# Quantized experts: two key and value banks in each of eight middle turns, copied by ScalarE, which also scales six tiles of tokens

## The chip, the cores and the metric

The kernel runs on one core of one Trainium2 chip. It is one program with one launch. The metric is device time in microseconds (us) of a whole execution, the median of several runs. A core has five engines that work side by side, each of which takes its own instructions in the order of the program: TensorE (PE in the profile, with its weight loads apart as PEld), VectorE (DVE), ScalarE (ACT), GpSimd (POOL) and SyncE (SP, which here only starts transfers). [...]

## The reference

Two decoder layers, each an attention-like block, a cross attention and a feed-forward block with a layer norm behind each. The change touches the first block of layer 0, a mixture of eight quantized experts plus one shared expert over 2048 tokens of width 256, and the place where some work of layer 1 (its keys and values) is done early.

```python
def activation_quant(x):
    scale = 127.0 / jnp.clip(jnp.max(jnp.abs(x), axis=-1, keepdims=True), 1e-05)
    return jnp.clip(jnp.round(x * scale), -128, 127) / scale
def weight_quant(w):
    scale = 1.0 / jnp.clip(jnp.mean(jnp.abs(w)), 1e-05)
    return jnp.clip(jnp.round(w * scale), -1, 1) / scale
def bitlinear(x, w):
    xn = rmsnorm(x, BIT_EPS)
    return activation_quant(xn) @ weight_quant(w).T
def bit_mlp(x, gate_proj_w, down_proj_w):
    gate, y = jnp.split(bitlinear(x, gate_proj_w), 2, axis=-1)
    return bitlinear(jax.nn.silu(gate) * y, down_proj_w)
# layer 0, first block
shared_out = bit_mlp(x_flat, shared_gate_w, shared_down_w)
...
routed = routed + w_keep[:, None] * bit_mlp(x_flat, expert_gate_w[e], expert_down_w[e])   # e in 0..7, top 2, capacity 320
# layer 1, cross attention, from the context alone
K = (key_value @ W_k); V = (key_value @ W_v)
```

(`activation_quant` and `weight_quant` stand in the reference inside a straight-through form, whose value is the one shown.)

## The kernel before

`stage0` computes the quantized experts. Its order is written out by hand (`manual_schedule`): every engine gets its instructions in the order in which the Python code calls them.

**Tiles and turns.** The stage works on 36 tiles of 128 token rows: 14 tiles of the shared expert, 20 of the routed experts (five for each pair of experts, gathered by an indirect transfer), and 2 more shared ones. The loop at L689 runs turns n = 0 to 37, and in one turn three tiles are in flight. In turn n:

- PE multiplies the tokens of tile n + 2 by the gate and up weights (`gated`, L503, into `ps_g` and `ps_y`, two buffers each), multiplies the hidden rows of tile n - 1 by the down weights (`down`, L557, into the single `ps_o`), and transposes the hidden rows of tile n (`turn`, L546, into `ps_t`, two buffers);
- ACT copies the transposed rows of tile n - 1 out (`turned`, L550, tile `m_hT`), computes silu for tile n + 1 (`silu`, L511, tile `m_sg`), and sums the squares of tile n (`squares`, L520);
- DVE multiplies silu by the other half (`hidden`, L516, tile `m_h`), takes the largest magnitude (L524), two small steps (L529, L530), rounds (`rounded`, L541, tile `m_r`), and writes tile n - 2 out (`done`, L564 or L570; ACT does it at L568 for odd expert tiles);
- the token rows of a new group are transposed by PE (L472) and copied by ACT (L473, tile `xqT`).

**Jobs.** Each turn also has a list of jobs, all of them behind the work above. Expert e is prepared in six of these turns from n = 2 + 3e on (`made_in`): sums of its weights on ACT (L223, L231) and DVE (L225), a small matmul (`total`, L235), scaling on ACT (L244), rounding on DVE (L247, L250). Turns 0 to 3 quantize token tiles 8 to 15, two tiles a turn, by `quantized` (L284 scales and rounds one tile into `m_q`, L285 writes it to `xq` as bf16). Turns 2 to 8 hold the pieces of the routing, a long row of small DVE instructions (L321 to L429).

**Banks of keys and values.** `made_early` (L575) is a generator. Each `next` on it gives PE one PSUM bank of layer 1's keys or values to compute (L2108 for the 16 key banks, L2115 for the 12 value banks, 28 in all), always into the same tile `ps_k`, of which there is one buffer (`bufs=1`). `out_of` (L583) copies the bank into a tile `kv` (L585) and SP sends that to DRAM (L586). In the loop, from turn 4 on, one bank a turn is made just ahead of `gated`, and its copy stands behind `down`: on ACT in turns 4 to 10 and where n % 3 is 1, on DVE in the other turns behind 10. The last bank is made in turn 31. The copy on ACT stands in program order behind `turned`, `silu` and `squares` of its turn.

Of the kernel before, what the change touches and what calls it, by code (L numbers as in the profile page):

```python
# [13 lines left out]
AF = mybir.ActivationFunctionType  # L14
ALU = mybir.AluOpType
# [9 lines left out]
MAGIC = 12582912.0  # L25
# [93 lines left out]
def stage0(K, early, ahead, late, late_dram, context):  # L119
# [6 lines left out]
    tc, nc = K.tc, K.nc  # L126
    x = K.x
    with ExitStack() as ctx:
# [21 lines left out]
        def load_half():  # L150
            what, i = halves[len(w_kv)]
            w_kv.append(K.new(wp, [P, KD, 512], F32, "w_kv", bufs=2))
            wide = K.ins["l1x_W_" + what].rearrange("(k p) n -> p k n", p=P)
            nc.sync.dma_start(w_kv[-1], wide[:, :, 512 * i:512 * i + 512])
# [9 lines left out]
        for g in range(4):  # L164
            t = K.new(wp, [P, KD, 4 * P], F32, "q", bufs=5)
# [9 lines left out]
        magic = K.new(keep, [P, 1], F32, "magic")  # L175
# [34 lines left out]
        def weights(e):  # L210
# [48 lines left out]
        ss, am, rs_bit, rs_gate, a, step, sc = (  # L259
            K.new(keep, [P, NB], F32, t) for t in ("ss", "am", "rs_bit", "rs_gate", "a", "step", "sc")  # L260
        )
# [19 lines left out]

        def quantized(b):
            t = K.new(work, [P, D], F32, "m_q", bufs=3)
            nc.vector.tensor_scalar(t, x[b], sc[:, b:b + 1], MAGIC, ALU.mult, ALU.add)  # L284
            nc.vector.tensor_scalar(xq[:, b, :D // 2].bitcast(BF16), t, MAGIC, None, ALU.subtract)  # L285


# [178 lines left out]
        def tokens(g, t0):  # L466

            m = min(4, g.n - t0)
            pt = K.new(ps, [P, 8, P], BF16, "ps_t")
            for t in range(m):  # L470
                for k in range(KD):
                    nc.tensor.transpose(pt[:, 2 * t + k, :], g.rows[t0 + t][:, k * P:(k + 1) * P], K.identb)  # L472
            return lambda: nc.scalar.copy(g.xqT[:, 2 * t0:2 * (t0 + m), :], pt[:, :2 * m, :])  # L473
# [18 lines left out]
        def scaled(g):  # L492
            nc.vector.tensor_tensor(g.s1, g.factor, g.backs[0], ALU.mult)
# [3 lines left out]
        def gated(n):  # L497
            g, t = tiles[n]
            pg[n], py[n] = (K.new(ps, [P, FF], F32, tag) for tag in ("ps_g", "ps_y"))
            for j, dst in enumerate((pg[n], py[n])):  # L500
                for part, w in g.use[t]:
                    for k in range(KD):
                        nc.tensor.matmul(  # L503
                            dst[part, :], g.xqT[:, 2 * t + k, part], w[0][:, k, FF * j:FF * j + FF],
                            start=(k == 0), stop=(k == KD - 1),
                        )

        def silu(n):
            g, t = tiles[n]
            sg[n] = K.new(work, [P, FF], F32, "m_sg", bufs=3)  # L510
            nc.scalar.activation(sg[n], pg[n], AF.Silu, scale=g.s1[:, t:t + 1])  # L511

        def hidden(n):
            g, t = tiles[n]
            h[n] = K.new(work, [P, FF], F32, "m_h", bufs=2)
            nc.vector.scalar_tensor_tensor(h[n], py[n], g.s1[:, t:t + 1], sg[n], ALU.mult, ALU.mult)  # L516

        def squares(n):
            g, t = tiles[n]
            nc.scalar.activation(sg[n], h[n], AF.Square, accum_out=g.ss[:, t:t + 1])  # L520

        def largest(n):
            g, t = tiles[n]
            nc.vector.tensor_reduce(g.am[:, t:t + 1], h[n], AX.X, ALU.max, apply_absolute_value=True)  # L524

        def step_of(n):
            g, t = tiles[n]
            at = slice(t, t + 1)
            nc.vector.tensor_scalar(g.step[:, at], g.am[:, at], 1e-9, 1.0 / 127.0, ALU.max, ALU.mult)  # L529
            nc.vector.reciprocal(g.s2[:, at], g.step[:, at])  # L530

        def factor(n):
            g, t = tiles[n]
            at = slice(t, t + 1)
            K.rsqrt(small, g.rs[:, at], g.ss[:, at], 1.0 / FF, 1e-8, "m_rt")
            nc.gpsimd.tensor_scalar(g.s3[:, at], g.rs[:, at], g.step[:, at], g.backs[1][:, at], ALU.mult, ALU.mult)

        def rounded(n):
            g, t = tiles[n]
            r[n] = K.new(work, [P, FF], F32, "m_r", bufs=2)  # L540
            nc.vector.tensor_scalar(r[n], h[n], g.s2[:, t:t + 1], MAGIC, ALU.mult, ALU.add)  # L541

        def turn(n):
            pt[n] = K.new(ps, [P, 4, P], F32, "ps_t")
            for k in range(4):
                nc.tensor.transpose(pt[n][:, k, :], r[n][:, k * P:(k + 1) * P], K.ident)  # L546

        def turned(n):
            hT[n] = K.new(work, [P, 4, P], BF16, "m_hT", bufs=3)
            nc.scalar.activation(hT[n], pt[n], AF.Identity, bias=unmagic)  # L550

        def down(n):
            g, t = tiles[n]
            po[n] = K.new(ps, [P, D], F32, "ps_o", bufs=1)
            for part, w in g.use[t]:
                for k in range(4):
                    nc.tensor.matmul(po[n][part, :], hT[n][:, k, part], w[1][:, k, :], start=(k == 0), stop=(k == 3))  # L557

        def done(n):
            g, t = tiles[n]  # L560
            s = g.s3[:, t:t + 1]
            if g.shared:
                b = g.i + t
                nc.vector.scalar_tensor_tensor(x[b], po[n], s, x[b], ALU.mult, ALU.add)  # L564
                return
            y = K.new(work, [P, D], F32, "y", bufs=3)
            if t % 2:
                nc.scalar.mul(y, po[n], s)  # L568
            else:
                nc.vector.tensor_scalar(y, po[n], s, None, ALU.mult)  # L570
            at = PAIR * g.i + P * t
            nc.sync.dma_start(y_dram[at:at + P, :], y)


        def made_early():  # L575
            for i in range(4):
                yield from context.early(
                    *halves[i], w_kv[i], ctxT, lambda: K.new(ps, [P, 512], F32, "ps_k", bufs=1),
                )
                if i < 2:  # L580
                    load_half()

        def out_of(bank, to, on_vector):  # L583
            t = K.new(work, [P, 512], F32, "kv", bufs=3)
            (nc.vector.tensor_copy if on_vector else nc.scalar.copy)(t, bank)  # L585
            nc.sync.dma_start(to, t)  # L586


# [5 lines left out]
        for b in range(4):  # L594
            quantized(b)
# [10 lines left out]
        for b in range(4, 8):  # L606
            quantized(b)
# [54 lines left out]
        for b in range(8, 12):  # L662
            job((b - 8) // 2, quantized, b)
# [21 lines left out]

        turned_tokens, made_banks = None, made_early()
        for n in range(N + 2):  # L689
            old, mid, now = 1 < n, 0 < n <= N, n < N  # L690
            if mid:
                turned(n - 1)
            if turned_tokens is not None:
                turned_tokens()
                turned_tokens = None
            if n in first_jobs:
                first_jobs[n]()
            if now:
                hidden(n)
            if n in then_jobs:  # L700
                then_jobs[n]()
            if n + 1 < N:
                silu(n + 1)
            if now:
                largest(n)
                squares(n)
                step_of(n)
                rounded(n)
            if old:
                done(n - 2)  # L710
            bank = next(made_banks, None) if n >= 4 else None
            if n + 2 < N:
                gated(n + 2)
            if mid:
                down(n - 1)
                factor(n - 1)
            if bank is not None:
                out_of(*bank, n > 10 and n % 3 != 1)
            for f, args in jobs.get(n, ()):
                f(*args)  # L720
            if n + 2 in starts:
                scaled(starts[n + 2])
            if n + 3 in starts:
                prepare(starts[n + 3])
                turned_tokens = tokens(starts[n + 3], 0)
            if n + 2 in starts and starts[n + 2].n > 4:
                turned_tokens = tokens(starts[n + 2], 4)
            if now:
                turn(n)
        assert next(made_banks, None) is None  # L730
# [2055 lines left out]
```

## Time and profile before

| what | value |
| --- | --- |
| median of 3 runs | 1367.72 us (1364.27 to 1368.48) |
| profiled execution, device time | 1373.0 us |
| its span, first to last instruction | 1371.2 us |
| stage of this change in the span | about 0 to 197 us |
| busy in the span | PE 89%, PEld 62%, DVE 60%, ACT 49%, POOL 35% |
| mean granted TensorE clock | 0.961 |
| bank copies (L585) | 14 on ACT, 8.2 us busy, 586 ns each; 14 on DVE, 9.5 us busy, 681 ns each |
| scaling of a token tile (L284) | 16 on DVE, 5.6 us busy, 348 ns each |

The turns can be found by the 36 `m_h` instructions of L516 on DVE: turn 0 begins at 23.81 us, turn 4 at 51.23, turn 9 at 84.02, turn 17 at 120.34, turn 24 at 150.88, turn 32 at 180.46 and turn 35 at 190.27. In a timeline a row gives start, length, engine, line, operation, what is written and read, how many instructions were merged, and in brackets how long the engine was idle before it and what ended that wait. The length of a row is longer than the distance to the next row of the same engine, since instructions are pipelined: for what an engine can do in a time, distances between starts count.

### The profile page before, as it was taken

How to read it: one execution, taken by the hardware profiler on the slowest of the kernel's cores; microseconds unless marked ns; L12 is line 12 of the kernel's file. 1: busy time of each engine (PE TensorE's matmuls, PEld its weight loads, DVE VectorE, ACT ScalarE, POOL GpSimd, SP SyncE). 2: the span in 40 equal slices, each digit the busy share in tenths (PEclk: the TensorE clock that was granted, in tenths of full speed). 3: DMA queues.
4: the chain of work that ended last, by engine and by line, in shares of the span. 5: the costliest groups of instructions: out<-in, count | busy, mean ns of one | idle time of the engine just before them, and what ended most of it. 6: DMA issues, size and time to landing. Idle time of an engine off the chain costs nothing.

```text
span 1371.2 us, 19329 instructions
## 1 busy us (share of the span) xinstructions
PE 1216.6 (89%) x6815; PEld 848.0 (62%) x6815; DVE 823.1 (60%) x1753; ACT 672.6 (49%) x1736; POOL 473.1 (35%) x632
## 2 busy tenths in 40 slices
PE   3678888889978898989798999998989999999994
PEld 1456444666654566766666888877776665666653
DVE  7799977989976898856555566676334111211115
ACT  5779864768965566636225566556431111111110
POOL 3256547658872566530052323323102000000003
PEclk9899988989999999989799999999999999999998
DMA  8458324201100311112000211210023322133002
GB/s 297 157 169 285 137 62 103 28 1 55 47 32 33 100 62 47 47 39 77 0 1 32 75 65 62 79 64 30 1 68 133 107 73 100 43 108 108 10 8 75
DMA packets 63121, 103.55 MB, mean 76 GB/s; under 512 B 11920, under 2 KB 41712, under 8 KB 62768
## 3 DMA queue, kind: packets, MB, share of 16 engines
q1 hardware_dynamic: 60848, 96.76, 20.8%
q0 software_dynamic: 2176, 5.55, 1.9%
q8 instruction: 54, 0.88, 0.3%
q14 instruction: 43, 0.35, 0.1%
HBM read 81.74 MB, written 16.35 MB: 72 GB/s over the span
## 4 chain that ended last, share of the span: by engine, by line
PE 55%; DVE 29%; ACT 7%; issue 4%; POOL 3%; DMA 2%; SPq 0%; DVEq 0%; POOLq 0%; ACTq 0%
PE ps_y L2616 8%; PE ps_m L2605 8%; PE ps_g L2605 7%; PE ps_m L2161 4%; DVE acc L1356 3%; ACT s L2263 2%; PE ps_t L2283 2%; PE ps_m L2292 2%; DVE cT L1365 2%; DVE m L2257 1%; DVE s L2253 1%; DVE s L915 1%; PE ps_t L2272 1%; PE ps_s L2250 1%; DVE m L922 1%
## 5 line engine op out<-in xcount | busy, mean ns | idle before, releaser
L2610 DVE TENSOR_TENSOR h<-h,ps_m 128x512 f32<-128x512 f32 x60 | 41.3, 688 | 228.4 <-PE ps_m L2605 228.4
L82 POOL TENSOR_SCALAR ln_t<-ln_mv 128x1 f32<-128x1 f32 (+2 forms) x76 | 15.0, 197 | 442.3 <-DVE ln_mv L90 296.2
L2263 ACT ACTIVATE s<-s,m 128x128 f32<-128x128 f32 x256 | 99.3, 390 | 69.0 <-DVE m L2257 69.0
L2609 ACT ACTIVATE h<-ps_g 128x512 f32<-128x512 f32 x60 | 35.8, 597 | 171.0 <-PE ps_g L2605 171.0
L2605 PE MATMUL ps_g<-xin,w 128*128 128x512 f32 x224 | 106.3, 592 | 0.0
L2605 PE MATMUL ps_m<-xin,w 128*128 128x512 f32 x224 | 105.3, 592 | 0.0
L2616 PE MATMUL ps_y<-w,h 128*128 128x256 f32 x448 | 97.8, 379 | 0.0
L2616 PEld LDWEIGHTS ps_y<-w,h 128*128 128x128 f32 x448 | 85.1, 190 | 14.6 <-issue 3.3
L2267 POOL TENSOR_TENSOR s<-s,t 128x1024 f32<-128x1024 f32 x32 | 60.7, 1898 | 86.7 <-DVE t L2266 86.7
L927 ACT ACTIVATE s<-s,m 128x128 f32<-128x128 f32 x256 | 83.2, 394 | 12.3 <-DVE m L922 12.3
L2605 PEld LDWEIGHTS ps_m<-xin,w 128*128 128x128 f32 x224 | 42.5, 190 | 51.4 <-issue 50.2
L2605 PEld LDWEIGHTS ps_g<-xin,w 128*128 128x128 f32 x224 | 42.0, 190 | 46.4 <-issue 45.0
L2161 PE MATMUL ps_m<-xT,half 128*128 128x256 f32 x256 | 62.7, 390 | 1.8 <-issue 1.3
L2617 ACT COPY y<-ps_y 128x256 f32<-128x256 f32 x30 | 11.2, 372 | 104.7 <-PE ps_y L2616 73.9
L2253 DVE TENSOR_TENSOR s<-ps_s,hide 128x1024 f32<-128x1024 f32 x32 | 39.1, 1223 | 36.1 <-PE ps_s L2250 36.0
L2292 PE MATMUL ps_m<-half,oT 128*128 128x256 f32 x256 | 59.3, 385 | 0.0
L1356 DVE SCALAR_TENSOR_TENSOR acc<-ps_m,l1a_conv_w,acc 128x508 f32<-128x508 f32 (+2 forms) x72 | 53.2, 739 | 3.0 <-ACT acc L1349 1.3
L2161 PEld LDWEIGHTS ps_m<-xT,half 128*128 128x128 f32 x256 | 47.7, 195 | 8.4 <-issue 2.0
L2292 PEld LDWEIGHTS ps_m<-half,oT 128*128 128x128 f32 x256 | 47.4, 190 | 7.5
L2263 ACT ACTIVATION_READ_ACCUMULATOR s<-s,m 128x1 f32 x256 | 48.1, 188 | 0.0
L83 POOL TENSOR_TENSOR ln_rs<-ln_t,mhalf 128x1 f32<-128x1 f32 (+2 forms) x76 | 45.6, 600 | 6.3
L1347 PE MATMUL ps_m<-xnT,l1a_in_proj 128*128 128x512 f32 x96 | 45.5, 596 | 0.4 <-ACT y L1317 0.4
(543 smaller groups left out, 3063.7 us busy)
## 6 DMA issues: line engine op xcount, KB each, us to landing
w<-in_w_gate_dram SPq DMA_DIRECT2D x9, 1024.0 KB, 7.2
csb<-cs_dram SPq DMA_DIRECT2D x16, 512.0 KB, 3.7
w<-in_l1f_gateT_dram SPq DMA_DIRECT2D x14, 512.0 KB, 4.4
w<-in_l1f_upT_dram SPq DMA_DIRECT2D x14, 512.0 KB, 5.8
w<-in_l1f_downT_dram SPq DMA_DIRECT2D x14, 512.0 KB, 4.7
k<-kv SPq DMA_DIRECT2D x20, 256.0 KB, 2.4
v<-kv SPq DMA_DIRECT2D x20, 256.0 KB, 2.1
ring<-k SPq DMA_DIRECT2D x10, 512.0 KB, 4.2
```

The source lines that it names most:

```text
L83: return self.nc.gpsimd.tensor_tensor(out, t, self.mhalf[: out.shape[0], :n], ALU.pow)
L927: nc.scalar.activation(at, at, AF.Exp, bias=m[h][:, i:i + 1])
L1347: nc.tensor.matmul(pc, w.inp[:, k, at:at + P], xnT[g][:, k, :], start=(k == 0), stop=(k == KD - 1))
L1356: nc.vector.scalar_tensor_tensor(accv[:, :, j:], pcv[:, :, :P - j], w.conv[:, c, TAPS - 1 - j:TAPS - j], accv[:, :, j:], ALU.mult, ALU.add,)
L2161: nc.tensor.matmul(pq[:, j, :], wt[k][:, at], src[:, k, :], start=(k == 0), stop=(k == KD - 1))
L2253: nc.vector.tensor_tensor(half(b, j), pss.rearrange("p r c k -> p (r c) k"), hide.unsqueeze(1).to_broadcast([P, 8, P]), ALU.add,)
L2263: nc.scalar.activation(at, at, AF.Exp, bias=m[j][:, i:i + 1], accum_out=t[j][:, i:i + 1])
L2267: nc.gpsimd.tensor_tensor(half(b, j), half(b, j), t[j].unsqueeze(2).to_broadcast([P, 8, P]), ALU.mult)
L2292: nc.tensor.matmul(py[b], oT[b][:, c, :], w.o[c // 4][:, c % 4, :], start=(c == 0), stop=(c == NC - 1))
L2605: nc.tensor.matmul(ps[:, j, :], m[k][:, c * P:(c + 1) * P], self.r.xin[:, k, e, cols], start=(k == 0), stop=(k == KD - 1),)
L2610: nc.vector.tensor_tensor(h, h, pu, ALU.mult)
L2616: nc.tensor.matmul(pd, rows(c), w.down[c // 4][:, c % 4, :], start=(c == 0), stop=(c == FI // P - 1))
```

## The change

Three things are changed.

1. `quantized` takes its first instruction (scale and round) to ACT for tiles 8, 9, 10, 11, 14 and 15. The second instruction, which reads its result, stays on DVE. Tiles 0 to 7, 12 and 13 are as before.
2. `out_of` always copies on ACT.
3. At the end of each of the turns 9 to 16, ahead of `turn(n)`, a second bank is made. Its copy stands in turn n + 1, on ACT, behind `squares` and `done` and ahead of that turn's first bank. The 28 banks end in turn 23.

```diff
         def quantized(b):
             t = K.new(work, [P, D], F32, "m_q", bufs=3)
-            nc.vector.tensor_scalar(t, x[b], sc[:, b:b + 1], MAGIC, ALU.mult, ALU.add)
+            if b < 8 or b in (12, 13):
+                nc.vector.tensor_scalar(t, x[b], sc[:, b:b + 1], MAGIC, ALU.mult, ALU.add)
+            else:
+                nc.scalar.activation(t, x[b], AF.Identity, scale=sc[:, b:b + 1], bias=magic)
             nc.vector.tensor_scalar(xq[:, b, :D // 2].bitcast(BF16), t, MAGIC, None, ALU.subtract)
-        def out_of(bank, to, on_vector):
+        def out_of(bank, to):
             t = K.new(work, [P, 512], F32, "kv", bufs=3)
-            (nc.vector.tensor_copy if on_vector else nc.scalar.copy)(t, bank)
+            nc.scalar.copy(t, bank)
             nc.sync.dma_start(to, t)
-        turned_tokens, made_banks = None, made_early()
+        turned_tokens, made_banks, more = None, made_early(), None
         for n in range(N + 2):
...
             if old:
                 done(n - 2)
+            if more is not None:
+                out_of(*more)
             bank = next(made_banks, None) if n >= 4 else None
             if n + 2 < N:
                 gated(n + 2)
             if mid:
                 down(n - 1)
                 factor(n - 1)
             if bank is not None:
-                out_of(*bank, n > 10 and n % 3 != 1)
+                out_of(*bank)
             for f, args in jobs.get(n, ()):
                 f(*args)
...
             if n + 2 in starts and starts[n + 2].n > 4:
                 turned_tokens = tokens(starts[n + 2], 4)
+            more = next(made_banks) if 9 <= n < 17 else None
             if now:
                 turn(n)
```

## The prediction

> **What bounds the stage now.** First the busy time of the engines in three stretches: turns 9 to 16, 17 to 23, 24 to 31.
>
> ```profile
> core 0: us, PE busy (x) PEld busy (x) DVE busy (x) ACT busy (x) POOL busy (x), PEclk, DMA share, GB/s
> 84.05:120.27 36.22, 31.63 (x193) 23.15 (x194) 34.29 (x78) 32.21 (x51) 24.59 (x45) 1.00 0.77 249
> 120.27:150.16 29.89, 26.83 (x150) 16.50 (x149) 28.51 (x64) 27.96 (x46) 17.43 (x34) 1.00 0.66 227
> 150.16:180.45 30.29, 28.18 (x143) 14.43 (x141) 28.67 (x63) 23.32 (x43) 15.50 (x35) 1.00 0.32 112
> ```
>
> DVE is 95% busy in each, but nobody has room: in turns 9 to 16 PE has 4.6 us free of 36.2 and ACT 4.0. Only behind 150 us has ACT slack (7.0 us). Next one turn in order of time, turn 15 (its `m_h` is at 111.39), with the row that follows on each engine:
>
> ```profile
> 110.67 1.89 PE L2108 MATMUL ps_k<-ctxT,w_kv 128*128 128x256 f32 x8
> 111.04 0.68 ACT L550 ACTIVATE m_hT<-ps_t,unmagic 128x512 bf16<-128x512 f32 x1
> 111.61 0.69 ACT L511 ACTIVATE m_sg<-ps_g,m_s 128x512 f32<-128x512 f32 x1
> 112.19 0.64 ACT L520 ACTIVATE m_sg<-m_h 128x512 f32<-128x512 f32 x1
> 112.40 0.59 PE L503 MATMUL ps_g<-q,xqT 128*128 128x512 bf16 x2
> 112.80 1.24 ACT L244 ACTIVATE w<-w,magic,w_s 128x1024 f32<-128x1024 f32 x1
> 112.83 0.59 PE L503 MATMUL ps_y<-q,xqT 128*128 128x512 bf16 x2
> 114.07 0.68 DVE L585 COPY kv<-ps_k 128x512 f32<-128x512 f32 x1
> 114.20 0.60 PE L557 MATMUL ps_o<-q_d,m_hT 128*128 128x256 bf16 x4 [0.77 <-DVE x L564]
> 114.63 0.60 PE L546 MATMUL ps_t<-ident,m_r 128*128 128x128 f32 x4
> 115.21 1.97 PE L2108 MATMUL ps_k<-ctxT,w_kv 128*128 128x256 f32 x8
> 115.27 0.69 ACT L550 ACTIVATE m_hT<-ps_t,unmagic 128x512 bf16<-128x512 f32 x1 [1.23 <-PE ps_t L546]
> 117.22 0.59 ACT L585 COPY kv<-ps_k 128x512 f32<-128x512 f32 x1
> ```
>
> The reader is to see that the bank is PE's first work of a turn. It starts 0.58 us behind the transposes of the turn before (114.63, then 115.21) and waits for nobody, because `ps_k` was emptied a whole bank's time earlier, at 114.07. The bank fills PE while ACT does `m_hT`, `m_sg` and the squares. The turn's length of 4.53 us (36.22 over 8) is DVE's.
>
> **Part 1, two banks a turn.** There is one `ps_k`. In the new order PE runs, in a turn: bank, `gated`, `down`, second bank, `turn`. ACT runs `turned`, `silu`, `squares`, copy of the second bank of the turn before, copy of this turn's bank, jobs. So PE's first bank of turn n waits for a copy that stands behind `squares(n)`, which stands behind `turned(n-1)`, which needs the transposes that PE does only behind the second bank. The two engines wait for each other in a ring, and what waits on PE behind that first bank is everything: `gated`, `down`, and so DVE and ACT of the next turn. Once round, in distances between starts from the rows above:
>
> - first bank 1.73 (110.67 to 112.40); `gated` 0.86 (twice 112.40 to 112.83); `down` 0.43 (114.20 to 114.63); second bank 1.73; `turn` until `turned` can start 0.64 (114.63 to 115.27): PE's part, 5.39 us;
> - `turned` 0.57, `silu` 0.58, `squares` with its read 0.61 (111.04, 111.61, 112.19, 112.80); the copy 0.59; release to PE 0.05 (114.15, the end of DVE's L564, to 114.20): ACT's part, 2.40 us, in which PE stands still.
>
> Together 7.79 us a turn. The second bank itself doesn't wait: ACT's copy of the first can start when the bank is 2.01 old (115.21 to 117.22) and ends at 2.60, PE comes to the second at 3.02. ACT's job (at most 2.0 us, L244) lies beside PE's `gated` to `turn`, and DVE (34.3 us for the eight turns) beside all of it; these are covered. Eight rounds, from the bank of turn 9 to that of turn 17, are 62.3 us. To it come pieces that now hide and then lie in the ring: copies of token rows on ACT (L473) in turns 10, 12, 13 and 17, by their distances 0.47, 0.89, 0.25, 0.89; their transposes on PE (L472) 0.22, 0.45, 0.12, 0.44; one `y` (L568) 0.36 in turn 17. Sum 4.1. So 66.4 us instead of 36.2: **+30.2 us**. Bounds: +6.6 if the waits vanished and PE's own 5.35 us a turn set it (2 x 1.73 + 0.86 + 0.43 + 0.44, and 0.15 for token rows; 8 x 5.35 - 36.2), and the +30.2, with some 3 us either way, if the ring holds. I take +30.2, because the program's order leaves no other way round.
>
> The transfers: each copy brings one to SP's queue (2.4 us to landing, 256 KB). A copy needs the `kv` buffer of three copies before, 1.5 turns or 11.7 us earlier. In turn 11 SP issues 14 loads for later stages in a row, which took 9.2 us (97.29 to 106.46 on SP); the second bank of that turn queues behind them, and 9.2 + 2.4 is just under 11.7. I cost it at 0; without that cover it is 1 us, once.
>
> **The clock.** A PE that waits may be slowed:
>
> ```profile
> 52.03 1.01 PE L503 MATMUL ps_y<-q_s,xqT 128*128 128x512 bf16 x2 [2.91 <-DVE m_h L516]
> 76.68 2.92 PE L2108 MATMUL ps_k<-ctxT,w_kv 128*128 128x256 f32 x8
> ```
>
> The first, behind a wait of 2.91 us, took 1.01 instead of 0.59. The second took 2.92 instead of 1.97 and had only waits of 1.68 and 1.76 us in the 5 us before. From 52 to 84 us PE was busy 22.52 of 32 and the granted clock was 0.85; from 84 to 120 it was 1.00. The ring leaves PE still 2.40 of 7.79 us, 31%, as much as the stretch at 0.85. Bounds for eight turns: 0, and 5.39/0.85 - 5.39 = 0.95 a turn, 7.6 us. I take **+4 us**, the middle, as the waits at 52 to 84 were uneven and some longer.
>
> [...]
>
> **Part 2, all copies on ACT.** 14 copies leave DVE, 0.60 each in distances (109.67 to 110.27), 8.4 us; 28 are now on ACT at 0.48 (117.22 to 117.70). Four of the moved ones stood in turns 11 to 16, where the ring decides: 0. Five stood in turns 17 to 23, and there ACT (27.96 of 29.89 busy) takes 5 x 0.48 = 2.4 for the 3.0 that DVE loses: I take 0, bounds -2.4 and +1.9. In turns 24 to 31 no bank is left, and DVE, which ran without a gap, loses five copies, 3.0, and the one wait of 0.41 us that a copy had for its bank (165.51): **-3.4 us**. The last turns have DVE's own row of work (2.36 us from 187.91 to 190.27) as a floor, which isn't reached.
>
> **Part 3, six tiles scaled on ACT.** DVE loses 6 x 0.39 = 2.3 us (26.38 to 26.75, 30.45 to 30.83). But DVE takes its instructions in order too, and the L285 that stays waits for ACT.
>
> ```profile
> 30.24 0.29 DVE L285 TENSOR_SCALAR xq<-m_q 128x256 bf16<-128x256 f32 x1
> 31.04 1.39 DVE L264 TENSOR_REDUCE am<-x 128x1 f32<-128x256 f32 x4
> 31.43 0.20 ACT L520 ACTIVATION_READ_ACCUMULATOR m_sg<-m_h 128x1 f32 x1
> 45.09 0.28 DVE L331 TENSOR_REDUCE best<-pr 128x16 f32<-128x128 f32 x1 [1.13 <-ACT pr L328]
> 48.05 0.19 ACT L520 ACTIVATION_READ_ACCUMULATOR m_sg<-m_h 128x1 f32 x1
> ```
>
> Turn 0: ACT is free at 26.24, both tiles are ready by 27.0, nothing lost. Turn 1: the scaling stands on ACT behind the squares (31.43). With ACT's 0.41 us for such a tile and 0.30 between two (L268 at 23.47), tile 11 is ready at 32.23, DVE's second L285 runs at 32.28 and L264 at 32.49 instead of 31.04: +1.45. DVE runs without a gap from 27.56 to the routing's first step at 36.69, and PE's next transposes wait for that step, so it stays. Turn 3: the scaling stands behind squares at 48.05, moved by the same 1.45 to 49.50; tile 15 is ready at 50.3, DVE goes on at 50.56, where L331 now starts at 45.09. Behind L331 DVE has the routing without a gap until the `m_h` at 51.23, for which PE and ACT wait. So **+5.5 us** in all; bounds -2.3 (ACT never late) and +6.5.
>
> **Sum.** 30.2 + 4.0 - 3.4 + 5.5 = +36.3. The profiled execution took 1373.0 (span 1371.2 and 1.8 around it), so 1409.3 for such a one; the median shown is 5.3 us lower, 1367.7, and the forecast goes by it: **1404 us**. All later stages need the stage's result and move along.
>
> **Rivals.**
> - *The engines' own work sets it, not the ring.* Turns 9 to 16 at PE's 5.35 us: +6.6, with +5.5 and -3.4 makes +8.7, 1376. For it: PE and ACT are nearly full already. Against: it needs ACT's copy ahead of `turned`, and it stands behind.
> - *Relief of DVE decides, and it is faster.* DVE was 95% busy; it loses 8.4 + 2.3 = 10.7 us: 1357. It decides if PE's idle time in turns 9 to 16 takes eight more banks, 8 x 1.73 = 13.8 us. Against: there were 4.6 us.
> - *The clock halves all through the ring.* PE's 5.39 us double: 8 x 5.39 = 43 instead of 4, 1443. For it: the row at 76.68. Against: from 59 to 84, with many waits of 1 to 2 us, only the 3.4 us around that bank were slow.
> - That the banks aren't doubled: the built order shows both, with the wait for ACT on each.
>
> **How the numbers follow.** Forecast 0.82, engines' work 0.08, clock 0.06, relief 0.04. Range: front +3.5 to +6.5, ring +27 to +32, clock 0 to +7.6, turns behind -5.8 to -1.5, together +25 to +45, that is 1392 to 1412; widened by the spread of the runs (1364.3 to 1368.5) and a little of the clock's case, 1390 to 1417. Within 0.3% (4 us), about what a measurement of this kernel can tell from no change, lies a quarter of the relief's case: same 0.01, faster 0.03, slower 0.96.
>
> **What would show it.** The bank of turn 17 some 66 us behind that of turn 9; PE's first bank of a turn with an idle time of 2.4 us ended by ACT `kv`; DVE idle in these turns, about 30 us more; `L331` near 50.5, behind a wait for ACT `m_q`; turns 24 to 31 about 3 us shorter. Wrong would be: no PE wait for `kv`, or a turn near 5.4 us.

## The result, and the profile after

| | before | after |
|---|---|---|
| median of 4 runs, us | 1368.10 (1364.27 to 1368.53) | 1410.80 (1408.22 to 1414.47) |
| ratio, 95% interval | | 1.0321 [1.0291, 1.0350] |
| profiled execution, us | 1373.0, span 1371.2 | 1410.84, span 1408.8 |
| bank of turn 9 starts, us | 84.05 | 89.62 |
| from there to the bank of turn 17 | 36.22 | 76.07 |
| from there to the transposes of turn 23 | 29.45 | 30.50 |
| from there to the transposes of turn 31 | 32.39 | 30.42 |
| from there to stage 1's first matmul | 15.54 | 15.37 |
| stage 1's first matmul starts, us | 197.65 | 241.98 |

The change made the kernel 42.7 us slower; 1404 had been forecast. The stage is 44.33 us longer in the two traces. Where stages 1 to 5 run the same instructions, they still differ from execution to execution: from stage 1's first matmul to the end of the span it is 1173.6 us before and 1166.8 after, and 1164.5 to 1176.4 over all twelve profiles of this study. A change of a few us inside this stage is therefore read at stage 1's first matmul (below: the end of the stage); the runs' times confirm it only when it is larger.

In the code after, a line behind L287 stands 3 lower and one behind the loop of turns' first edit up to 6 lower than before: the bank's copy is L588, `turn` L549, `turned` L553, `silu` L514, `squares` L523, `hidden` L519, a bank L2114 or L2121. The busy time by stretch of the kernel after, with the columns as before, for turns 9 to 16, 17 to 23 and 24 to 31:

```profile
89.62:165.69 76.07, 54.48 (x236) 35.75 (x236) 37.53 (x83) 41.82 (x69) 24.86 (x47) 0.88 0.56 174
165.69:196.62 30.93, 29.42 (x136) 15.34 (x137) 21.83 (x50) 26.69 (x45) 16.39 (x33) 0.91 0.45 151
196.62:225.81 29.19, 18.52 (x118) 10.90 (x116) 25.51 (x58) 22.51 (x41) 13.96 (x35) 0.88 0.17 53
```

DVE, 95% busy before, is busy for 37.53 of 76.07 us in the first stretch, and no engine is full there: PE has 72%, ACT 55%. A stretch in which everybody has time is one in which they wait for each other. PE's clock fell from 1.00 to 0.88 in the same rows. The round of turn 15 in order of time, on PE and ACT (start, length, engine, line; in brackets the idle time before):

```profile
143.20 0.60 PE L549 MATMUL ps_t<-ident,m_r 128*128 128x128 f32 x4
143.84 0.69 ACT L553 ACTIVATE m_hT<-ps_t,unmagic 128x512 bf16<-128x512 f32 x1 [1.45 <-PE ps_t L549]
144.42 0.68 ACT L514 ACTIVATE m_sg<-ps_g,m_s 128x512 f32<-128x512 f32 x1
144.99 0.63 ACT L523 ACTIVATE m_sg<-m_h 128x512 f32<-128x512 f32 x1
...
145.60 0.58 ACT L588 COPY kv<-ps_k 128x512 f32<-128x512 f32 x1
146.24 2.50 PE L2121 MATMUL ps_k<-w_kv,ctxT 128*128 128x512 f32 x4 [2.44 <-ACT kv L588]
148.53 1.06 PE L506 MATMUL ps_g<-q,xqT 128*128 128x512 bf16 x2
...
149.38 1.06 PE L506 MATMUL ps_y<-q,xqT 128*128 128x512 bf16 x2
150.23 0.97 PE L560 MATMUL ps_o<-q_d,m_hT 128*128 128x256 bf16 x4
151.04 1.88 PE L2121 MATMUL ps_k<-w_kv,ctxT 128*128 128x512 f32 x4
152.76 0.60 PE L549 MATMUL ps_t<-ident,m_r 128*128 128x128 f32 x4
```

ACT's wait ends with PE's transposes, and PE's wait ends with ACT's copy: the ring. What ACT does between (143.84 to 146.24) are 2.40 us, in which PE stands still. Soon behind the wait PE works at half speed (the granted clock is 0.50 from 147.57 to 150.98): from 148.53 to 149.38 are 0.85 us for `ps_g`, where the same two matmuls need 0.43 elsewhere, and the bank of 146.24 takes 2.29 us, where the one of 107.99, behind an equal wait but at full clock, took 1.83. That is the second part of the loss.

The waits of the same kernel from 89 to 166 us (waiting engine, line, for whom: total, times, longest); before, PE had no wait for `kv` in these turns:

```profile
PE ps_k L2114 <- ACT kv L588: 11.6, 5, 3.4
PE ps_k L2121 <- ACT kv L588: 8.5, 3, 3.7
```

Part 3 of the change, on ACT and DVE in turns 1 and 3:

```profile
30.20 0.20 ACT L523 ACTIVATION_READ_ACCUMULATOR m_sg<-m_h 128x1 f32 x1
30.29 1.08 ACT L287 ACTIVATE m_q<-x,magic,sc 128x256 f32<-128x256 f32 x2
30.92 0.29 DVE L288 TENSOR_SCALAR xq<-m_q 128x256 bf16<-128x256 f32 x1 [1.51 <-ACT m_q L287]
...
49.16 1.08 ACT L287 ACTIVATE m_q<-x,magic,sc 128x256 f32<-128x256 f32 x2
49.78 0.29 DVE L288 TENSOR_SCALAR xq<-m_q 128x256 bf16<-128x256 f32 x1 [5.99 <-ACT m_q L287]
...
50.51 0.27 DVE L334 TENSOR_REDUCE best<-pr 128x16 f32<-128x128 f32 x1
```

DVE stands before L288 until ACT, whose scaling is queued behind the squares, has delivered. The routing's L334 begins at 50.51; it began at 45.09.

### The profile page after: what moved, and what is told of

The parts are those of the page before. It is cut to its first block, busy times and chain, and to the rows that moved or that the text cites. A ratio compares the mean times of both kernels' runs of the same rounds, so it can differ in the third digit from the quotient of the medians.

```text
span 1408.8 us, 19332 instructions
## 1 busy us (share of the span) xinstructions
PE 1226.5 (87%) x6815; PEld 853.1 (61%) x6815; DVE 813.4 (58%) x1733; ACT 682.7 (48%) x1756; POOL 470.3 (33%) x632
## 4 chain that ended last, share of the span: by engine, by line
PE 51%; DVE 21%; ACT 8%; issue 4%; POOL 3%; DMA 1%; DVEq 0%; POOLq 0%; ACTq 0%
PE ps_y L2622 7%; PE ps_m L2611 7%; PE ps_g L2611 7%; PE ps_m L2167 4%; DVE acc L1362 3%; ACT s L2269 2%; PE ps_t L2289 2%; PE ps_m L2298 2%; DVE cT L1371 2%; DVE m L2263 1%; DVE s L2259 1%; DVE s L921 1%; PE ps_t L2278 1%; PE ps_s L2256 1%; PE ps_g L1986 1%
## 5 line engine op out<-in xcount | busy, mean ns | idle before, releaser
L2114 PE MATMUL ps_k<-ctxT,w_kv 128*128 128x256 f32 x128 | 39.3, 462 | 11.6 <-ACT kv L588 11.6
```

What stands on the lines that cost most here:

```text
L2114: nc.tensor.matmul(bank[:, 2 * P * j:2 * P * (j + 1)], w[:, k, cols], ctxT[:, k, G * g * P:G * (g + 1) * P], start=(k == 0), stop=(k == KD ...
```

## The experiments

Theory: three things cost time. The ring (PE's first bank of a turn behind a copy that stands late in ACT's order), PE's half clock behind the ring's waits, and the scaling that makes DVE wait for ACT. Rivals: too much work for some engine, a clock that has nothing to do with the waits, or transfers.

| kernel | median, us (lowest to highest) | kernel before, same chip | ratio, 95% interval | bank of turn 9 | to bank of turn 17 | clock in that stretch | end of the stage |
|---|---|---|---|---|---|---|---|
| before | | | | 84.05 | 36.22 | 1.00 | 197.65 |
| after | 1410.80 | 1368.10 | 1.0321 [1.0291, 1.0350] | 89.62 | 76.07 | 0.88 | 241.98 |
| e1 | 1377.38 (1370.66 to 1381.91) | 1370.23 | 1.0046 [1.0021, 1.0070] | 91.48 | 36.41 | | 205.42 |
| e2 | 1369.42 (1366.44 to 1373.33) | 1370.23 | 1.0001 [0.9979, 1.0023] | 82.75 | 35.34 | 1.00 | 195.70 |
| e3 | 1410.46 (1402.07 to 1413.21) | 1371.28 | 1.0276 [1.0228, 1.0325] | 84.18 | 77.53 | 0.86 | 238.16 |
| e4 | 1389.24 (1385.44 to 1397.84) | 1370.23 | 1.0158 [1.0116, 1.0200] | 90.65 | 53.41 | 0.97 | 218.91 |
| e5 | 1396.93 (1388.31 to 1398.47) | 1370.23 | 1.0172 [1.0131, 1.0214] | 88.45 | 58.77 | 1.00 | 220.03 |
| e6 | 1411.11 (1407.60 to 1411.92) | 1371.28 | 1.0304 [1.0261, 1.0347] | 89.98 | 74.27 | 1.00 | 237.76 |
| e8 | 1385.92 (1379.50 to 1386.70) | 1371.28 | 1.0108 [1.0070, 1.0145] | 90.08 | 48.96 | 1.00 | 213.86 |
| e9 | 1367.93 (1366.07 to 1370.81) | 1371.28 | 0.9983 [0.9961, 1.0005] | 84.03 | 36.44 | 1.00 | 196.93 |
| e10 | 1402.20 (1400.10 to 1405.20) | 1370.60 | 1.0233 [1.0211, 1.0256] | 90.11 | 67.89 | 1.00 | 230.94 |
| e11 | 1405.92 (1405.07 to 1406.66) | 1370.60 | 1.0256 [1.0239, 1.0273] | 89.71 | 67.89 | 1.00 | 232.71 |

**e1, the scaling alone.** The kernel before, with the first hunk of the diff and nothing else.

> The kernel before with only the scaling of tiles 8 to 11, 14 and 15 on ScalarE; banks and copies as before. Theory (VectorE takes its instructions in order and waits for ScalarE): the m_h of turn 4 comes 5.4 us later than the 51.23 of before, and the whole is 5.5 us slower, 1373.6 against 1368.1. Rival (VectorE is the bound and is relieved of six instructions): 2.3 us faster, 1365.8.

Measured: 0.46% slower, [+0.21, +0.70], that is 2.9 to 9.6 us, and the end of the stage 7.8 us later, 7.4 of them by the bank of turn 9 (5.57 in the kernel after). DVE waits 2.16 us for `m_q` in turn 1 and 5.99 in turn 3. The `m_h` of turn 4 comes at 58.63, 7.40 us later where 5.4 was expected; in the kernel after it is 5.38. One pair of profiles is not good to better than some 3 us here: up to the bank of turn 9 all kernels with the scaling run the same instructions, and so do those without, and that bank comes between 88.45 and 91.48 us in the eight profiles with it and between 82.75 and 84.18 in the four without. The means are 6.3 us apart. So the scaling costs somewhat more than the theory asked, though it takes work from the fullest engine.

**e2, the copies alone.** The kernel before, with all copies on ACT, still one bank a turn.

```diff
-                out_of(*bank, n > 10 and n % 3 != 1)
+                out_of(*bank, False)
```

> The kernel before with all 28 bank copies on ScalarE and still one bank a turn. Theory: no ring can form, since a bank is copied in its own turn and the next one starts a turn later, so VectorE's relief counts where ScalarE has room: 1 to 5 us faster, 1363 to 1367 against 1368.1, most of it behind turn 24. Rival (ScalarE is the bound of the middle turns, and copies there cost as much as they relieve): within 2 us of before, or slower.

Measured: no difference within 0.23%, which is 3.2 us, so a gain of 1 or 2 us is neither shown nor excluded. In its trace the stage ends 2 us earlier, but 1.3 of them are there at the bank of turn 9, ahead of anything that was changed. ACT is 32.00 of 32.00 us busy from 118 to 150: what DVE lost there, ACT became. As a cause of the slowdown the copies are out.

**e4, the second bank's copy at once.** The kernel after, with this copy behind its own bank instead of a turn later.

```diff
-            if more is not None:
-                out_of(*more)
...
-            more = next(made_banks) if 9 <= n < 17 else None
+            if 9 <= n < 17:
+                out_of(*next(made_banks))
```

> The changed kernel with one call moved: the second bank's copy is called right behind its matmuls, so on ScalarE it stands ahead of the next turn's m_hT instead of behind its squares. Same work on every engine. Theory (a ring of waits between TensorE and ScalarE): a turn of 9 to 16 falls from 9.5 us to about 5.7 (5.39 of TensorE and a wait of 0.48), eight turns with the token rows about 47 us instead of 76, the whole 1382 against 1410.8. Rival (two banks a turn are simply too much work for TensorE or ScalarE): no gain, above 1405.

Measured: 21.6 us below the kernel after, with the same work on every engine. So it was not too much work; it was one copy's place in ACT's order. A turn is 5.72 us where nothing else happens (97.59 to 103.31), and PE waits 0.2 to 0.3 us for a copy. But 47 us for the eight turns and 1382 for the whole had been expected, and 53.41 and 1389.24 came. One turn stood out, in the timeline of this kernel:

```profile
112.33 2.83 SPq L75 DMA_DIRECT2D dist_scale<-in_dist_scale_dram  x1
117.49 4.64 SPq L589 DMA_DIRECT2D k<-kv  x4
121.20 0.58 ACT L588 COPY kv<-ps_k 128x512 f32<-128x512 f32 x1 [3.74 <-DMA k<-kv]
121.84 3.60 PE L2113 MATMUL ps_k<-ctxT,w_kv 128*128 128x256 f32 x8 [2.27 <-ACT kv L588]
```

SP issues turn 11's 14 loads one after another (to 117.49, one of them 2.83 us); the copies' transfers queue behind them, and ACT's copy has no free `kv` buffer until one lands. With turns of 7.79 us three copies were 11.7 us, enough; with 5.7 us they are 8.6, and the cover is gone. PE then waits 2.27 us and the bank takes 3.60 us, where the others of these turns take 1.88 to 1.99.

**e8, the same with five buffers.** `bufs=3` in `out_of` becomes `bufs=5`.

> The kernel in which the second bank is copied right behind its own matmuls (1389.24 us), with five buffers instead of three for the copies on their way to memory. Theory (one copy there waited 3.74 us for the transfer of three copies before, held up behind fourteen loads on SyncE's queue, and TensorE then 2.27 us and a bank at half clock): no such wait, no slow bank, bank of turn 9 to bank of turn 17 in 46 to 50 us beside 53.41, the run 1383 to 1387 us. Rival (the wait only moves, or ScalarE's own work is the bound there): 52 us or more, the run at 1388 or above.

Measured: no wait for a transfer, no slow row, 48.96 instead of 53.41 us for the eight turns, and a median 3.3 us lower, all as expected. The times alone would not show it, since the intervals of the two ratios overlap; the traces settle the cause of that one stall.

**e5, the copy one place behind `turned`.** The kernel after, with the copy of the second bank moved ahead of `silu` and `squares`, but still in the next turn.

```diff
             if turned_tokens is not None:
                 turned_tokens()
                 turned_tokens = None
+            if more is not None:
+                out_of(*more)
...
-            if more is not None:
-                out_of(*more)
```

> The changed kernel with the second bank's copy moved only ahead of silu and squares, still behind m_hT and the token rows. Theory: the ring's part on ScalarE falls from 2.40 to about 1.21 us (0.57 + 0.59 + 0.05), 8 x 1.19 = 9.5 us less, and with shorter waits most of the 8.7 us of half clock goes too: 1392 to 1398 against 1410.8. Rival (too much work): no gain, above 1405.

Measured: in the expected range. In rounds without token rows PE waits 1.25 us, 1.15 to 1.19 less than 2.40 to 2.44, which is `silu` and `squares` (0.57 and 0.61); a turn is 6.70 us (125.49 to 132.19). And there is not one slow row in the ring, not even behind the 2.17 us of turn 12:

```profile
110.89 1.99 PE L2114 MATMUL ps_k<-ctxT,w_kv 128*128 128x256 f32 x8 [2.17 <-ACT kv L588]
132.19 1.99 PE L2121 MATMUL ps_k<-w_kv,ctxT 128*128 128x512 f32 x4 [1.25 <-ACT kv L588]
```

**e6, PE kept busy while it waits.** The kernel after, with four f32 matmuls ahead of the first bank in turns 10 to 17. They go into `ps_g`, and `gated` overwrites them.

```diff
             if more is not None:
                 out_of(*more)
+            if more is not None:
+                pg[n + 2] = K.new(ps, [P, FF], F32, "ps_g")
+                for k in range(4):
+                    nc.tensor.matmul(pg[n + 2], K.ones, ctxT[:, k % KD, :FF], start=(k == 0), stop=(k == 3))
```

> The changed kernel with four idle f32 matmuls (what they write is overwritten by the gate's product) put in front of the first bank in turns 10 to 17, into the gate's PSUM tile that is free by then: some 1.73 us of work inside TensorE's wait of 2.4 us for the second bank's copy, so that the wait should fall to about 0.7 us and the ring should keep its length of 7.79 us. Theory (about 8.7 us of the ring's 76.07 are TensorE at half its clock behind its own idle time): no or few slow rows of the bank, turns of 7.8 us, bank of turn 9 to bank of turn 17 in 65 to 69 us, the run 1400 to 1405 us beside 1410.8. Rival (the half clock comes from TensorE's load or from elsewhere, not from its gaps): slow rows as many as before or more, 74 us or more, the run at 1408 us or above.

Measured: the time of the kernel after, but for another reason. I had mis-sized the filler: it takes 3.44 us, not 1.73 (105.58 to 109.02 us in its timeline), fills the whole wait and lengthens a turn without token rows to 8.62. Yet there is no slow row left and the granted clock is 1.00, with more work than before. By time the test is inconclusive; by the clock the rival has fallen.

**e10, a filler that fits.** The same with two matmuls.

> The changed kernel with two idle f32 matmuls in TensorE's wait in place of four (four took 3.44 us, more than the wait, and lengthened each turn to 8.62 us; two take 1.72 by that row). Theory (TensorE's half clock in the ring is the price of its own idle time): TensorE waits some 0.7 us for the second bank's copy, no or few slow rows, granted clock of the ring 0.97 or more, turns of 7.8 us, bank of turn 9 to bank of turn 17 in 65 to 69 us instead of 76.07, stage 1's first matmul at 231 to 236 us instead of 241.98, the run 1400 to 1405 us. Rival (slow rows come whatever TensorE does, and the run with four matmuls had none by luck): granted clock below 0.93, 72 us or more, the run at 1408 or above.

Measured: as expected; only the end of the stage, 230.94 us, lies 0.06 ahead of its range. The stretch of turns 9 to 16 of this kernel, and one round of it on PE:

```profile
90.11:158.00 67.89, 59.84 (x264) 36.70 (x268) 37.33 (x83) 41.79 (x69) 25.13 (x47) 1.00 0.61 193
```

```profile
137.20 0.60 PE L551 MATMUL ps_t<-ident,m_r 128*128 128x128 f32 x4
137.63 1.88 PE L721 MATMUL ps_g<-ctxT,ones 128*128 128x512 f32 x4
...
140.24 1.98 PE L2127 MATMUL ps_k<-w_kv,ctxT 128*128 128x512 f32 x4 [0.72 <-ACT kv L590]
```

PE begins the idle work (L721) right behind the transposes and still waits 0.72 us for the copy: the ring has its length of 7.89 us (132.35 to 140.24), but the bank no longer runs slow. The eight turns are 8.18 us shorter than after, the end of the stage comes 11.04 us earlier, and the run is 8.6 us faster by medians taken on two chips (the intervals of the two ratios do not overlap). Work that nobody needs made the kernel faster.

**e11, half of it.** One matmul, 0.86 us.

> The same with one idle matmul, 0.86 us, so that a wait of some 1.55 us is left in a turn of 7.8 us (TensorE busy 80 per cent; it was 69 in the changed kernel and 81, with waits of 1.25 us, where the copy stood behind the turned tokens and the clock was 1.00). Theory A (the share of idle time decides): clock 0.97 or more, the ring in 65 to 69 us, the run as with two matmuls within 2 us. Theory B (a wait above some 1.5 us is enough, whatever the share): slow rows again, clock below 0.95, the ring in 70 us or more.

Measured: for the ring as in theory A, not B. With waits of 0.59 to 1.58 us in six rounds, and 2.49 in one, the clock stays at 1.00 and the eight turns take 67.89 us. Behind the last and longest wait the bank of turn 17 is slow:

```profile
115.71 1.99 PE L2120 MATMUL ps_k<-ctxT,w_kv 128*128 128x256 f32 x8 [2.49 <-ACT kv L590]
157.60 2.77 PE L2127 MATMUL ps_k<-w_kv,ctxT 128*128 128x512 f32 x4 [2.85 <-ACT kv L590]
```

Which idle time decides is not shown. The run is 3.7 us above e10, not within 2; 1.8 of it is there at the end of the stage.

**e3, the change without its scaling.**

> The changed kernel with all sixteen tiles scaled by VectorE as before; banks and copies as changed. Theory (the parts add up; the scaling alone cost 5.5 us at the turn it is in): bank of turn 9 some 5.5 us earlier than the changed kernel's 89.62, the ring still 74 to 78 us, the run 1403 to 1407 us. Rival (ScalarE is what is full, and the two parts share one cost): the ring shorter, the run below 1398, or the scaling hidden behind the ring, the run at 1410.

Measured: by time a miss, 1410.46, no less than the kernel after. The bank of turn 9 is 5.44 us earlier, as expected; the ring is 1.46 longer, with the clock at 0.86 instead of 0.88 (six slow stretches ahead of the last wait, not five), the end of the stage 3.8 earlier, and the stages behind took 6.4 us more in this profile than in that of after. The four runs spread from 1402.07 to 1413.21; the gain is seen in the trace and not shown in time.

**e9, only the late copies on ACT.** The kernel before, with `10 < n < 24 and n % 3 != 1` in the call of `out_of`.

> The kernel before with ScalarE's copies in turns 24 to 31 alone (the turns up to 23 as before, no second bank, no scaling moved). Theory (VectorE is full in the late turns, and each of its copies there is worth some 0.4 us; in the turns 17 to 23 ScalarE becomes the bound): 1.5 to 3.5 us faster than the kernel before. Rival (VectorE's copies there lie beside other waits): within 0.5 us of it.

Measured: 0.17% faster, with an interval that reaches from 0.39% faster to 0.05% slower. In its trace the turns 24 to 31 lose 0.62 us, not 2, and DVE has new waits for ACT's `m_sg`, 1.6 us. By its interval it may beat the kernel before, as e2 may, and for neither is it shown.

## Why the prediction was right, and which term was mis-sized

- **The ring** was the mechanism, and its working held. One line was misread on the way, without weight for the sum: `ps_k` is not emptied a whole bank's time ahead, for the copy of 114.07 takes 0.68 us and is done some 0.5 us ahead of the bank of 115.21. PE waits 2.44 us (2.40 predicted), a turn without token rows is 7.80 to 7.91 us in e10 (7.79), and with the clock's part taken away by the filler of e10 the eight turns are 67.89 us (66.4): +31.7 where +30.2 had been taken. Most of the difference are the pieces of turns 10, 12, 13 and 17: the rounds that hold them take 8.78, 9.31, 8.44 and 9.88 in e10, together 5.2 above 7.79 apiece, not 4.1. e4, e5 and e8 show what it hangs on: the same banks and the same copies, moved up in ACT's order, are 14 to 25 us cheaper.
- **The clock** is the step that was mis-sized: 4 us taken, bounds 0 to 7.6, and 8.2 us measured in the ring (76.07 less 67.89), 11.0 to the end of the stage. The price was worked out as PE's 5.39 us divided by a mean clock of 0.85, as if the half clock fell evenly on PE's work and its waits. It falls on the work. In the ring of the kernel after, a mean of 0.88 over 76.07 us is about 18 us at half clock (0.12 x 2 x 76.07). Against their lengths at full clock (1.83 for a bank behind a wait, 0.43 for the others) the slow rows lost 8.2 us, so some 16 of those 18 us were matmuls, and the loss is what the filler of e10 took away. In the five half-clock stretches ahead of the last wait (last section) PE is busy for 16.60 of 17.05 us. The rival of a clock halved all through (1443) was wrong too: three of the nine first banks, those at 89.62, 107.99 and 155.80, and the rows up to the next wait are at a clock of 1.00.
- **The scaling**: 5.5 us taken, 5.57 measured at the bank of turn 9, 5.44 between e3 and the kernel after. L334 came at 50.51 (50.56 predicted). That it fits to 0.1 us is luck: over all profiles the difference is 6.3 us, inside the bounds, with a spread of 3 (see e1).
- **All copies on ACT**: 3.4 us less taken for turns 24 to 31, 1.97 found after, 3.04 in e10. DVE is nearly full there and waits 1.99 us in these turns of the kernel after (for `m_sg` 1.33 in two waits, for a total of weights 0.66), 1.02 in e10 and 0.41 before; that is most of the difference between the two. Both kernels have a slow stretch there. In the kernel after it falls on the transposed token rows (208.95 to 210.78, in a half clock from 209.01 to 215.84), and `m_sg` behind them comes late, a wait of 1.01; in e10 the slow rows lie ahead of them (192.10 to 198.53; 1.06 us where 0.59 is usual), and the same wait is 0.36. So part of what was missing is the clock again. How the rest divides wasn't tried. For the turns 17 to 23, 0 was taken: +1.05 after, where the bank at 165.69 took 3.78 us, and -1.24 in e10, inside the bounds of -2.4 to +1.9.
- **The transfers** cost nothing in the kernel after, as taken; the condition named there, three copies in 11.7 us, failed in e4 at 8.6.
- **The sum**: at the end of the stage +44.33 where +36.3 stood. The kernel e10 is at +33.3, and the prediction without its 4 at +32.3. The 11.0 us between the kernel after and e10 are 8.2 in the ring, 2.3 in turns 17 to 23 (the slow bank of 165.69 and the rows behind it), 1.1 in turns 24 to 31, and -0.5 ahead of turn 9, which is chance. So the clock makes most of the 8 us that the stage lies above its forecast. The medians differ by 42.7, 6.4 more than forecast; that they still lie inside the range, though the clock's term went above its bound of 7.6, is owed to the room that the bounds of the other terms had left.

## What to carry to other kernels

When one PSUM buffer is used twice in a turn, the copy that empties it belongs right behind its producer in the copying engine's order: what stands ahead of it in that queue is added to the turn of every engine that waits (here 2.40 us a turn; without `silu` and `squares` ahead, in e5, 1.15 to 1.19 less). An engine at 95% says where a gain would have to come from, not that relief of it helps (e1 took work from DVE and was 0.46% slower); the ring's length is got by going round it once, in distances between starts. Put the clock's loss on the work behind a wait: here a round with half clock was up to 1.77 us longer (next section). Idle matmuls in the wait are a quick test of how much of a stretch is the clock (e10: 8.18 of 76.07 us).

## What the hardware showed that was not expected

Waits of the same length did not cost the same. The first banks that waited for a copy in the kernel after, the stretch near each in which the granted clock was 0.50, and the round up to the next of these banks beside the same round of e10:

| bank at, us | wait, us | clock 0.50, us | round after, us | same round in e10, us |
| --- | --- | --- | --- | --- |
| 98.41 | 1.77 | 99.78 to 103.19 | 9.58 | 7.91 |
| 107.99 | 2.44 | none | 9.31 | 9.31 |
| 117.30 | 3.35 | 116.85 to 120.26 | 9.79 | 8.44 |
| 127.09 | 1.55 | 127.09 to 130.50 | 9.57 | 7.80 |
| 136.66 | 2.44 | 137.33 to 140.74 | 9.58 | 7.89 |
| 146.24 | 2.44 | 147.57 to 150.98 | 9.56 | 7.88 |
| 155.80 | 2.32 | none | 9.89 | 9.88 |
| 165.69 | 3.72 | 164.64 to 171.46 | | |

The five rounds with half clock are 1.35 to 1.77 us longer than those of e10, whose clock is 1.00; the two without are 0.00 and 0.01 longer. This is also why equal rounds of the ring came out unequal. Three waits of 2.44 us stand in the table, one without half clock. In the other kernels the bank behind 2.17 us in e5 (110.89) and the one behind 2.49 us in e11 (115.71) took 1.99 us, as at full clock, and the one behind 2.27 us in e4 (121.84) took 3.60. So the length of a wait doesn't settle it: 1.55 us had half clock with it, 2.49 had not. Nor does PE's share of a long stretch: over its eight turns PE is busy for 90% in e4, with a slow bank, and for 79% in e5, with none. What does settle it is not shown by these runs.
